# Seven quarter products in place of the full product in a projection, and where the conversions beside it run

## The chip, the cores and the metric

One core of a Trainium2 chip runs the whole program. Five engines work side by side on it: TensorE (PE, matrix products), VectorE (DVE, elementwise work and sums), ScalarE (ACT, activations and copies), GpSimd (POOL) and SyncE (SP, which only issues transfers here). Time is device time in microseconds (us) of one execution, the median of several.

## The reference

Two layers of attention over images of 512 channels and 32x32 = 1024 positions, for a batch of 8, all in 32-bit floating point:

```python
# layer 0: 8 heads
h = group_norm(xf, gn_w, gn_b)
q, k, v = split(einsum('oc,bct->bot', qkv_w, h) + qkv_b)   # per head
q, k, v = fake_quant(q), fake_quant(k), fake_quant(v)      # 8 bits, over the whole tensor
a = softmax(q * k * scale) @ v
x = xf + einsum('oc,bct->bot', proj_w, a) + proj_b         # the projection that is changed
# layer 1: 1 head of 512 channels
h = group_norm(x); q, k, v = h @ wq, h @ wk, h @ wv
x = x + (softmax(q k / sqrt(512)) v) wp + bp
```

## The kernel before, in words

A first stage (to about 570 us) computes q, k and v of layer 0 and their extremes. The rest is one long second stage. Its order is written out by hand: `attention()` is a generator that walks through layer 0's attention, image by image (8), pair of heads by pair (4), half of the positions by half (2) and 128 keys at a time (8); four such steps, called units, are one "advance". `others()` does for each image b the projection of layer 0 (`project`, line 1296), the group norm of layer 1 (`norm1`, line 1344) and layer 1's attention (`layer1`), and yields at chosen places; at each yield one advance of layer 0's attention is put between. So layer 0 of image b+2 runs beside layer 1 of image b. The instructions of TensorE, VectorE and ScalarE keep the order in which the program emits them. Nearly all of them are recorded under two helper lines: L209 is `mm`, every matmul, and L91 is the call through which every VectorE and ScalarE instruction goes; so groups are told apart by tile names.

In each unit TensorE makes scores (tile `st`, two PSUM banks), ScalarE takes their exponential (`pt`, 128x1024), one engine converts it to 16 bits (`two`), VectorE subtracts to get the low part (the other half of `two`, the group `two<-pt,two`), and TensorE multiplies both with v (`av`) and sums them (`sm`). For images after the first, the conversion is done on GpSimd for every fourth unit (line 1092) and on ScalarE for the rest. There are four `pt` buffers, so the exponential of unit u waits for the subtraction of unit u-4. An advance at u runs the products of units u to u+3 and the scores of units u+6 to u+9.

Work on VectorE that has time is put off by a small planner (`InOrder`, lines 89 to 157): `later` queues a chore under a name with a cost, a time when it is ready and one when it is due; `do` emits work that is wanted now, and first fills the gap before it with chores that fit; `settle` and `need` emit a chore at once because someone wants it. A chore is passed over if it would end more than 0.15 us after the gap:

```python
if begin + cost > limit + 0.15:
    continue
def elements(n):
    return 0.21 + n * 0.957e-3
```

`elements(512)` is 0.700 us, `elements(1024)` 1.190 us; a matmul of 256 columns counts 0.429 us. These figures only decide the order; the chip keeps its own time.

`project(b)` multiplies the 512x512 weights (tile `wp`) with image b's attention output (`ao`, four tiles of 128 channels x 2 halves x 512 positions). Per half it makes four outputs of 128 channels, each of four 128x128 by 128x512 products accumulated in one bank (`pj`); VectorE adds bank, bias and the input x into the tile `h` (`evict`), takes the statistics for layer 1's group norm (`stats`, a chore named "pj"), and SP stores the piece. Between the two halves lies one advance. For b = 0 the projection stands alone; for b = 1 to 7 it is put inside layer 1 of image b-1, in `o_run` (line 1540) after its fourth product, through `first` (line 1773): an advance ("the advance before"), half 0, an advance ("the middle one"), half 1, an advance in another order ("the late one": products of the first two units, then scores), then the norm. At b = 7 no attention is left, so the halves follow each other directly. In this place the banks `pj` are taken from the two buffers that the scores use (`score_bank`, line 315).

The norm averages over groups with a small matmul (`gps_b<-gmv_b,gavg`), which `more` (line 1781) emits right behind the fifth product of `o_run`, and a second one (`gps_b<-gd_b,gavg`) behind the sixth.

`seven` (line 1393) is the kernel's product by quarters in Winograd's form of Strassen's scheme: a product of 2x2 blocks with seven block products instead of eight, and sums of blocks before and after. Layer 1 uses it everywhere: tiles `g`, `v2ps`, `s` and `o` in the profile are its banks, two at a time, and each block product here is a number of 128x128 by 128x256 matmuls. `load_wp` (line 1266) fetches the projection's weights on ScalarE's queue, followed there by the image's x.

Of the kernel before, what the change touches and what calls it, by code (L numbers as in the profile page):

```python
# [18 lines left out]
P = 128  # L19
B, C, HH, WW = 8, 512, 32, 32  # L20
T = HH * WW
CC = C // P
# [36 lines left out]
def attn_pair_kernel(  # L59
# [166 lines left out]


    def norm_steps(
        src, dst, wcol, bank, nm, ccs=range(CC), fine=False, put=None, mv=None, apply=None
    ):  # L230

        n, c0 = len(ccs), ccs[0]
        put = put or (lambda hf, cost, work: work())
        if mv is None:
            st, mv = stat_tiles(n, nm)
            for i, cc in enumerate(ccs):
                for hf in range(NH):
                    dve.bn_stats(st[:, i, hf, :], src(cc, hf))  # L240
                aggregate(mv, st, i)
                if fine and i + 1 < n:
                    yield
        yield
        ps = bank(f"gps_{nm}")[:, 0:n]
        mm(ps, lhsT=gavg, rhs=mv[:, :, 0], start=True, stop=True)

        d = small.tile([P, n], F32, tag=f"gd{n}", name=f"gd_{nm}")
        mean = small.tile([P, n], F32, tag=f"gmean{n}", name=f"gmean_{nm}")

        def offsets():
            dve.tensor_sub(d, mv[:, :, 0], ps)
            dve.tensor_copy(mean, ps)
# [13 lines left out]
        if apply is not None:  # L267
            off = small.tile([P, n], F32, tag=f"goff{n}", name=f"goff_{nm}")
            dve.scalar_tensor_tensor(off, mean, -1.0, rstd, ALU.mult, ALU.mult)
            for i, cc in enumerate(ccs):  # L270
                apply(cc, rstd[:, i : i + 1], off[:, i : i + 1])
                yield
            return
        for hf in range(NH):
            for i, cc in enumerate(ccs):
                put(hf, 0.5, lambda i=i, cc=cc, hf=hf: dve.tensor_scalar(
                    dst(cc, hf), src(cc, hf), mean[:, i : i + 1], rstd[:, i : i + 1],
                    ALU.subtract, ALU.mult,
                ))
                if fine and i % 2 == 1:  # L280
                    yield
        if not fine:
            yield
# [23 lines left out]
    with ExitStack() as fast:  # L307
# [710 lines left out]
        def attention():  # L1018
# [44 lines left out]
            def split(u):  # L1063

                b, j, hf, s = units[u]
                pt, there = pts.pop(u)
                if not InOrder.planned:
                    for v in [v for v in put_off if v < u - 2]:
                        put_off.pop(v)()
                    deal(u)  # L1070
                else:
                    for v in list(put_off):
                        at_hand.add(v)
                        dve.later("sum", elements(1024), put_off.pop(v), pe.t, 9.0)
                if plain(b, s):
                    parts[u], ready[u] = pt, there
                    return
                two = partp.tile([P, 2, 2, 512], F16, tag="two", name=f"two_{b}_{j}_{hf}_{s}")
                parts[u] = two

                def rest():
                    dve.tensor_tensor(two[:, 1], pt, two[:, 0], ALU.subtract)
                    ready[u] = dve.t

                if u < BY_DMA and s in CAST_BY_DMA:
                    nc.gpsimd.dma_start(two[:, 0], pt)
                    put_off[u] = rest
                    return

                def cast(copy=act.copy):  # L1090
                    at_hand.add(u)
                    copy(two[:, 0], pt)  # L1092
# [64 lines left out]
            def finish(b, j, hf, u):  # L1157
# [106 lines left out]
                dma(xts[b][:, :, bass.ts(hf, 512)], x_v[b, :, :, bass.ts(hf, 512)])  # L1264

        def load_wp(b, dma):
            wps[b] = l2p.tile([P, CC, C], F32, tag="sums", name=f"wp0_{b}")
            dma(wps[b], w_sq[WP0])

        def load_first(u):  # L1270

# [21 lines left out]
            for t, src in zip(wm_tiles(b), wm_d):  # L1293
                act.dma_start(t, src)

        def project(b, bank=bank):

            settle("ao")  # L1300
            st, mvs[b] = stat_tiles(CC, f"b{b}")
            wp0 = wps.pop(b)
            for hf in range(NH):
                for oc in range(CC):
                    ps = bank(f"pj_{b}_{hf}_{oc}")
                    for cc in range(CC):
                        mm(
                            ps, lhsT=wp0[:, cc, bass.ts(oc, P)], rhs=ao[b, cc][:, hf, :],
                            start=(cc == 0), stop=(cc == CC - 1),
                        )  # L1310
# [33 lines left out]
        def norm1(b, bank=bank):  # L1344
# [14 lines left out]
                    put(hf, elements(512), work)  # L1359

            for n, _ in enumerate(norm_steps(
                at, at, V_GN1W, bank, f"b{b}", put=put, mv=mvs[b]
            )):
                if n == 2:
                    sums[b] = l2p.tile(
                        [P, 3, NH, CC // 2, 256], F32, tag="sums", name=f"sums2_{b}"
                    )
# [22 lines left out]
            dve.later("o", 0.25, spread, pe.t + 4.0, 5.0)  # L1390
            return rs

        def seven(nm, pairs, keep, whole, add, bank=bank):

            nonlocal turn
            turn ^= 1  # L1400
            x, y = (bank(f"{nm}_{i}").rearrange("p (t n) -> p t n", t=2) for i in range(2))

            def product(n, ps, start):
                left, right = pairs[n]
                k = left.shape[1]
                for t in range(2):
                    for i in range(k):
                        mm(
                            ps[:, t, :], lhsT=left[:, i, bass.ts(t, P)], rhs=right[:, i, :],
                            start=start and t == 0 and i == 0, stop=(i == k - 1),  # L1410
                            skip_group_check=True,
                        )
# [4 lines left out]
                (5, x, False, whole, None),  # L1417
            )
            for i, (n, ps, start, out, m) in enumerate(work):
                awaits(free[(i + turn) % 2])  # L1420
                product(n, ps, start)
                free[(i + turn) % 2] = out(ps) if m is None else out(m, ps)
                yield i + 1

        free = [0.0, 0.0]
        turn = 0

        def slots(gq):
# [235 lines left out]
        def layer1(b, steps):  # L1664
# [46 lines left out]
            for hf in range(NH):  # L1711
# [59 lines left out]
                if b + 1 < B and last:  # L1771

                    def first():
                        nonlocal ahead
                        yield -1
                        yield from project(b + 1, score_bank)
                        yield 2
                        ahead = norm1(b + 1, score_bank)
                        next(ahead)

                    def more():
                        next(ahead)
                        yield from ()

                    between = [first, more, more]
# [3 lines left out]
        def fold():  # L1789
# [36 lines left out]
            for i, (rows, lw, rw) in enumerate(((wa_rows, NQ1, NK1), (wm_rows, NV1, WP1))):  # L1826
# [74 lines left out]
        done = 0  # L1901
        dense = True
        late = False

        def advance():
            nonlocal done
# [407 lines left out]
```

## Time and profile before

| | |
|---|---|
| Median of 3 runs | 2557.06 us (2555.32 to 2558.21) |
| The profiled execution's own time | 2557.22 us |
| Its span, first to last instruction | 2555.4 us |
| Around the span | 1.8 us |
| TensorE busy | 2516.6 us (98%) |
| VectorE busy | 1895.6 us (74%) |
| ScalarE busy | 1348.2 us (53%) |
| GpSimd busy | 187.9 us (7%) |
| Mean granted TensorE clock | 0.999 |

Each row of the costliest groups reads: source line, engine, operation, output tile <- input tiles, shapes, count, then busy time and mean ns of one instruction, then how long the engine was idle just before these instructions and who ended that idle time. A 32-bit matmul stands in the trace as two instructions. Matmuls overlap, so busy time divided by the count is the spacing, and the mean of one is longer. The timeline merges neighbouring instructions of the same kind: start, duration, what, and in brackets the idle time before. The image b = 1 is taken as the sample: its projection starts at 930.9 us.

### The profile page before, as it was taken

How to read it: one execution, taken by the hardware profiler on the slowest of the kernel's cores; microseconds unless marked ns; L12 is line 12 of the kernel's file. 1: busy time of each engine (PE TensorE's matmuls, PEld its weight loads, DVE VectorE, ACT ScalarE, POOL GpSimd, SP SyncE). 2: the span in 40 equal slices, each digit the busy share in tenths (PEclk: the TensorE clock that was granted, in tenths of full speed). 3: DMA queues.
4: the chain of work that ended last, by engine and by line, in shares of the span. 5: the costliest groups of instructions: out<-in, count | busy, mean ns of one | idle time of the engine just before them, and what ended most of it. 6: DMA issues, size and time to landing. Idle time of an engine off the chain costs nothing.

```text
span 2555.4 us, 38727 instructions
## 1 busy us (share of the span) xinstructions
PE 2516.6 (98%) x15670; PEld 1746.1 (68%) x15670; DVE 1895.6 (74%) x2746; ACT 1348.2 (53%) x1687; POOL 187.9 (7%) x167
## 2 busy tenths in 40 slices
PE   8999999999999999999999999999999999999998
PEld 4788888873357756775777577657756775777687
DVE  7888776668887778777877787777778777775544
ACT  3332223219856655665667466656665675664122
POOL 0000000001100001000100100010101000100000
PEclk9999999999999999999999999999999999999999
DMA  4533333236622232223223222322232123212211
GB/s 167 178 142 124 132 124 121 110 130 164 164 88 63 79 113 87 59 70 127 92 59 104 84 87 74 109 96 63 80 109 91 55 72 124 87 51 84 87 38 39
DMA packets 160718, 250.70 MB, mean 98 GB/s; under 512 B 27153, under 2 KB 93713, under 8 KB 159121
## 3 DMA queue, kind: packets, MB, share of 16 engines
q1 hardware_dynamic: 125792, 182.81, 21.9%
q10 hardware_dynamic: 30560, 57.71, 6.6%
q0 software_dynamic: 4176, 7.60, 1.7%
q8 instruction: 125, 2.05, 0.3%
q14 instruction: 65, 0.52, 0.1%
HBM read 153.64 MB, written 86.28 MB: 94 GB/s over the span
## 4 chain that ended last, share of the span: by engine, by line
PE 85%; DVE 4%; issue 3%; ACT 2%; DMA 1%; POOL 0%; SPq 0%; ACTq 0%; DVEq 0%; POOLq 0%
PE s L209 15%; PE o L209 13%; PE qkps L209 12%; PE pj L209 8%; PE av L209 8%; PE v2ps L209 7%; PE g L209 6%; PE vps L209 6%; PE st L209 4%; PE sm L209 3%; ACT pt L91 1%; DVE two L91 1%; DVE h L91 1%; PE fold L209 0%; DVE acc L91 0%
## 5 line engine op out<-in xcount | busy, mean ns | idle before, releaser
L91 ACT ACTIVATE pt<-st,esc 128x1024 f32<-128x1024 f32 x467 | 497.1, 1115 | 332.7 <-PE st L209 316.8
L91 DVE TENSOR_TENSOR two<-pt,two 128x1024 f16<-128x1024 f32 x467 | 561.9, 1217 | 131.5 <-POOL two L1092 100.8
L91 ACT CAST two<-pt 128x1024 f16<-128x1024 f32 x346 | 350.8, 1056 | 6.9 <-ACT p L91 5.1
L1092 POOL CAST two<-pt 128x1024 f16<-128x1024 f32 x112 | 147.5, 1317 | 1406.8 <-PE sm L209 745.1
L209 PE MATMUL av<-two,v 128*32 128x512 f16 x3968 | 245.7, 381 | 2.5 <-DVE two L91 2.4
L209 PE MATMUL s<-g,h 128*128 128x256 f32 x1024 | 233.4, 380 | 0.0
L209 PE MATMUL pj<-ao,wp 128*128 128x512 f32 x512 | 224.0, 595 | 0.6 <-DVE h L91 0.6
L209 PEld LDWEIGHTS s<-g,h 128*128 128x128 f32 x1024 | 192.9, 190 | 31.0 <-issue 4.3
L91 ACT ACTIVATE u_ring<-qkps,qkbt 128x512 f32<-128x512 f32 x89 | 61.1, 687 | 243.6 <-PE qkps L209 228.9
L209 PEld LDWEIGHTS <-v 128*32 128x32 f16 x3968 | 92.0, 96 | 139.8 <-issue 66.7
L209 PEld LDWEIGHTS pj<-ao,wp 128*128 128x128 f32 x512 | 96.0, 190 | 122.5 <-issue 112.2
L209 PE MATMUL s<-g,sums 128*128 128x256 f32 x768 | 178.4, 381 | 0.2 <-DVE p L91 0.2
L209 PE MATMUL o<-p,v 128*128 128x256 f32 x768 | 175.2, 382 | 1.0 <-DVE p L91 1.0
L209 PE MATMUL st<-q,k 64*128 64x512 bf16 x1024 | 163.4, 382 | 12.2 <-ACT pt L91 7.8
L209 PEld LDWEIGHTS o<-p,v 128*128 128x128 f32 x768 | 144.3, 190 | 27.1 <-issue 5.7
L209 PEld LDWEIGHTS s<-g,sums 128*128 128x128 f32 x768 | 144.6, 190 | 24.3 <-issue 4.6
L209 PE MATMUL sm<-two,ones 128*32 128x512 f16 x1984 | 136.0, 379 | 0.0
L209 PEld LDWEIGHTS <-k 64*128 64x128 bf16 x1024 | 34.8, 94 | 144.1 <-issue 142.5
L209 PE MATMUL qkps<-half,w_high 128*128 128x512 f32 x480 | 132.5, 398 | 0.0
L209 PE MATMUL qkps<-half,w_mix 128*128 128x512 f32 x480 | 130.6, 394 | 1.0 <-DVE half L91 1.0
L209 PE MATMUL qkps<-half,w_low 128*128 128x512 f32 x480 | 130.5, 394 | 0.0
L209 PE MATMUL v2ps<-wm,h 128*128 128x256 f32 x512 | 119.9, 383 | 1.9 <-ACT g L91 1.3
(228 smaller groups left out, 3903.9 us busy)
## 6 DMA issues: line engine op xcount, KB each, us to landing
rs<-rs_d SPq DMA_DIRECT2D x76, 256.0 KB
x<-in_x_dram SPq DMA_DIRECT2D x32, 512.0 KB
q_d<-wa SPq DMA_DIRECT2D x32, 512.0 KB
k_d<-wa SPq DMA_DIRECT2D x32, 512.0 KB
v_d<-v_ring SPq DMA_DIRECT2D x32, 512.0 KB
raw<-q_d SPq DMA_DIRECT2D x32, 512.0 KB
raw<-k_d SPq DMA_DIRECT2D x32, 512.0 KB
x_d<-h SPq DMA_DIRECT2D x64, 256.0 KB
```

The costliest lines, as they stand in the source:

```text
L91: ins = self.latest = op(*args, **kw).ins
L209: ins = nc.tensor.matmul(ps, lhsT=lhsT, rhs=rhs, **kw).ins
L1092: copy(two[:, 0], pt)
```

## The change

For images 1 to 7 the projection is made by `seven` (`project_seven`); image 0 keeps the full product. While image 0 is projected, the four block sums of the weights are computed once (`combine_wp`) and all seven blocks are stored in device memory (`wp_d`). Later images load six blocks in one transfer into the buffer where the full weights stood (1.5 MB in place of 1 MB), and the seventh into a free part of layer 1's tile `v` (256 KB, on SP); that free part also takes two of the sums of the attention output. The other sums are formed in place in `ao`: one of them as a chore after the division of the second pair of heads (`first_sums`), the rest within each half. Each of the seven products is added by VectorE straight into the tile of x. The statistics are no longer settled at the end of the projection but after the late advance. The bias is taken out of the adding step: the norm's means are shifted by it (one small VectorE instruction more, ahead of the first averaging matmul) and it is added to layer 1's output bias. While the projection of images 1 to 6 runs, every fourth unit's conversion goes to ScalarE and not to GpSimd.

```diff
@@ norm_steps
+        if shift is not None:
+            dve.tensor_add(mv[:, :, 0], mv[:, :, 0], shift)
         ps = bank(f"gps_{nm}")[:, 0:n]
         mm(ps, lhsT=gavg, rhs=mv[:, :, 0], start=True, stop=True)
...
@@ split
-                elif s % 4 == 2:
+                elif s % 4 == 2 and not projecting:
                     cast(nc.gpsimd.tensor_copy)
...
@@ divide
                     dve.scalar_tensor_tensor(aot, aot, scl[:, 2:3], rs, ALU.mult, ALU.mult)
+                    if b and j == 1:
+                        first_sums(b)
...
@@ load_wp
-            wps[b] = l2p.tile([P, CC, C], F32, tag="sums", name=f"wp0_{b}")
-            dma(wps[b], w_sq[WP0])
+            wps[b] = w = l2p.tile([P, 6, CC // 2, C // 2], F32, tag="sums", name=f"wp0_{b}")
+            dma(w, wp_d[:, 0:6])
...
+        def first_sums(b):
+            for cc in range(CC // 2):
+                h = ao[b, cc]
+                dve.later("at", elements(512), lambda h=h: tt(
+                    h[:, :, 256:512], h[:, :, 256:512], h[:, :, 0:256], ALU.subtract
+                ), within=30.0)
+
+        def project_seven(b, room):
+            nonlocal projecting
+            projecting = True
+            settle("at")
             settle("ao")
...
+            nc.sync.dma_start(s4, wp_d[:, 6])
...
+            for k in range(2):
+                dve.do(elements(512), lambda k=k: second(k))
+
+            for hf in range(NH):
...
+                for step in seven(
+                    f"pj_{b}_{hf}",
+                    ((a11, h11), (a12, h21), (s2, th), (s3, h11), (s1, t1), (s4, h22), (a22, h21)),
+                    lambda n, ps: keeps[n](ps), into(q12, 0, 1, 1), lambda n, ps: adds[n](ps),
+                    score_bank, True,
+                ):
+                    if step in (1, 2):
+                        for k in range(2):
+                            h = (h11, h21)[step - 1][k]
+                            args = (h, th[k], h) if step == 1 else (h, h, th[k])
+                            dve.do(elements(256), lambda args=args: tt(*args, ALU.subtract))
+                    for oc in {6: (2, 3), 7: (0, 1)}.get(step, ()):
+                        dve.later("pj", 0.62 + 0.2 * hf, lambda oc=oc, stats=stats: stats(oc), within=4.0)
+                    chore()
+                if hf + 1 < NH:
+                    yield -1
...
@@ project (image 0)
-                        dve.scalar_tensor_tensor(
-                            xx, ps, vec[:, V_PB0 + oc : V_PB0 + oc + 1], xx, ALU.add, ALU.add
-                        )
+                        dve.tensor_tensor(xx, ps, xx, ALU.add)
...
@@ first, more
-                        yield from project(b + 1, score_bank)
+                        yield from project(b + 1, vt)
                         yield 2
+                        settle("pj")
                         ahead = norm1(b + 1, score_bank)
                         next(ahead)
...
                         next(ahead)
+                        projecting = False
...
@@ fold
                     dve.tensor_add(dst, tot, vec[:, V_BP : V_BP + CC])
+                    dve.tensor_add(dst, dst, vec[:, V_PB0 : V_PB0 + CC])
```

In `seven` the products come in the order 0, 1, 2, 3, 4, 6, 5 of the list, alternately into two banks x and y, beginning and ending with x. With the new argument `alone` its bank order starts afresh each time.

More of the change, by code (lines that the diff above doesn't have):

```diff
@@ L228, in norm_steps @@
     def norm_steps(
-        src, dst, wcol, bank, nm, ccs=range(CC), fine=False, put=None, mv=None, apply=None
+        src, dst, wcol, bank, nm, ccs=range(CC), fine=False, put=None, mv=None, apply=None,
+        shift=None,
     ):
@@ L252, in offsets @@
             dve.tensor_sub(d, mv[:, :, 0], ps)
-            dve.tensor_copy(mean, ps)
+            if shift is None:
+                dve.tensor_copy(mean, ps)
+            else:
+                dve.tensor_sub(mean, ps, shift)
             dve.tensor_mul(d, d, d)
@@ L1294, in load_wm, with combine_wp, keep @@
                 act.dma_start(t, src)
-        def project(b, bank=bank):
-            settle("ao")
+        wp_d = dram.tile([P, 7, CC // 2, C // 2], F32, tag="wp", name="wp_d")
+        def combine_wp():
+            wc = l2p.tile([P, 3, NT // 2, 256], F32, tag="vsum", name="wp_combined").rearrange(
+                "p a (s k) n -> p (a s) k n", k=2
+            )
+            a11, a12, a21, a22 = (
+                wps[0][:, k * CC // 2 : (k + 1) * CC // 2, m * 256 : (m + 1) * 256]
+                for m in range(2) for k in range(2)
+            )
+            s2, s3, s1, s4 = (wc[:, i] for i in range(4))
+            for args in (
+                (s1, a21, a22, ALU.add), (s2, s1, a11, ALU.subtract),
+                (s3, a11, a21, ALU.subtract), (s4, a12, s2, ALU.subtract),
+            ):
+                dve.later("wc", elements(512), lambda args=args: tt(*args), within=20.0)
+            def keep():
+                nc.sync.dma_start(wp_d[:, 3:7], wc[:, 0:4])
+            dve.later("wc", 0.0, keep, within=20.0)
+            nc.sync.dma_start(wp_d[:, 0], a11)
+            nc.sync.dma_start(wp_d[:, 1], a12)
+            nc.sync.dma_start(wp_d[:, 2], a22)
@@ new lines, in first_sums, with second, into, add @@
+        def first_sums(b):
[8 more added lines that the diff above has]
+            settle("at")
+            settle("ao")
+            st, mvs[b] = stat_tiles(CC, f"b{b}")
+            w = wps.pop(b)
+            a11, a12, a22, s2, s3, s1 = (w[:, i] for i in range(6))
+            t2 = room[:, 0 : NT // 2, 0:256].rearrange("p (k h) n -> p k h n", h=NH)
+            s4 = room[:, NT // 2 : NT // 2 + 2, 0:256]
+            nc.sync.dma_start(s4, wp_d[:, 6])
+            left, right = slice(0, 256), slice(256, 512)
+            def second(k):
+                tt(t2[:, k], ao[b, 2 + k][:, :, right], ao[b, k][:, :, right], ALU.subtract)
+            for k in range(2):
+                dve.do(elements(512), lambda k=k: second(k))
+            for hf in range(NH):
+                h11, t1, h21, h22 = (
+                    [ao[b, c + k][:, hf, n] for k in range(2)] for c in (0, 2) for n in (left, right)
+                )
+                th = [t2[:, k, hf] for k in range(2)]
+                q11, q12, q21, q22 = quarters(b, hf)
+                def into(q, row, col, full, hf=hf):
+                    def add(ps):
+                        there = dve.do(elements(512), lambda: tt(q, ps, q, ALU.add))
+                        if full is not None:
+                            nc.sync.dma_start(x1_d[b][row][hf][:, :, col * 256 : (col + 1) * 256], q)
+                        return there
+                    return add
+                def stats(oc, hf=hf):
+                    dve.bn_stats(st[:, oc, hf, :], xts[b][:, oc, bass.ts(hf, 512)])
+                    if hf == NH - 1:
+                        aggregate(mvs[b], st, oc)
+                keeps = [into(q, *at_, None) for q, at_ in ((q11, (0, 0)), (q21, (1, 0)), (q22, (1, 1)))]
+                adds = [into(q, *at_, 1) for q, at_ in ((q11, (0, 0)), (q21, (1, 0)), (q22, (1, 1)))]
+                for step in seven(
[3 more added lines that the diff above has]
+                    score_bank, True,
+                ):
+                    if step in (1, 2):
[8 more added lines that the diff above has]
+                    yield -1
+            for k in [k for k in ao if k[0] == b]:
+                del ao[k]
@@ L1301, in project @@
+        def project(b, room=None):
+            if b:
+                yield from project_seven(b, room)
+                return
+            settle("ao")
+            combine_wp()
             st, mvs[b] = stat_tiles(CC, f"b{b}")
@@ L1361, in norm1 @@
             for n, _ in enumerate(norm_steps(
-                at, at, V_GN1W, bank, f"b{b}", put=put, mv=mvs[b]
+                at, at, V_GN1W, bank, f"b{b}", put=put, mv=mvs[b], shift=vec[:, V_PB0 : V_PB0 + CC]
             )):
                 if n == 2:
+                    if b == 0:
+                        settle("wc")
                     sums[b] = l2p.tile(
@@ L1391, in inverse1, with seven @@
             return rs
-        def seven(nm, pairs, keep, whole, add, bank=bank):
+        def seven(nm, pairs, keep, whole, add, bank=bank, alone=False):
             nonlocal turn
-            turn ^= 1
+            turn ^= not alone
+            free, side = ([0.0, 0.0], 0) if alone else (busy, turn)
             x, y = (bank(f"{nm}_{i}").rearrange("p (t n) -> p t n", t=2) for i in range(2))
@@ L1408, in product @@
                         mm(
-                            ps[:, t, :], lhsT=left[:, i, bass.ts(t, P)], rhs=right[:, i, :],
+                            ps[:, t, :], lhsT=left[:, i, bass.ts(t, P)],
+                            rhs=right[i] if type(right) is list else right[:, i, :],
                             start=start and t == 0 and i == 0, stop=(i == k - 1),
@@ L1419, in seven @@
             for i, (n, ps, start, out, m) in enumerate(work):
-                awaits(free[(i + turn) % 2])
+                if not alone:
+                    side = turn
+                awaits(free[(i + side) % 2])
                 product(n, ps, start)
-                free[(i + turn) % 2] = out(ps) if m is None else out(m, ps)
+                free[(i + side) % 2] = out(ps) if m is None else out(m, ps)
                 yield i + 1
-        free = [0.0, 0.0]
+        busy = [0.0, 0.0]
         turn = 0
@@ L1781, in more @@
                     def more():
+                        nonlocal projecting
                         next(ahead)
+                        projecting = False
                         yield from ()
@@ L1903, in attn_pair_kernel @@
         late = False
+        projecting = False
         def advance():
```

## The prediction

> **What bounds the kernel now.** I read the engine totals and the chain that ended last first, then the groups of the projection, then the timeline around one projection (image 1).
>
> ```profile
> PE 2516.6 (98%) x15670; PEld 1746.1 (68%) x15670; DVE 1895.6 (74%) x2746; ACT 1348.2 (53%) x1687; POOL 187.9 (7%) x167
> ...
> L209 PE MATMUL pj<-ao,wp 128*128 128x512 f32 x512 | 224.0, 595 | 0.6 <-DVE h L91 0.6
> ```
>
> TensorE is busy 98% and the chain gives it 85%: less matmul time is less span, as long as TensorE is kept fed. The projections hold 224.0 us, 14.00 us for each of 16 halves. VectorE has 26% left on average, but the question is how much it has left there. So the timeline, TensorE first, image 1 (start, duration, what, idle before):
>
> ```profile
> 930.91 14.00 PE L209 MATMUL pj<-ao,wp 128*128 128x512 f32 x32
> 944.84 0.39 PE L209 MATMUL st<-q,k 64*128 64x512 bf16 x2
> 945.75 0.39 PE L209 MATMUL st<-q,k 64*128 64x512 bf16 x2 [0.52 <-DVE h L91]
> ...
> 947.49 0.60 PE L209 MATMUL st<-q,k 64*128 64x512 bf16 x4
> ...
> 963.36 1.05 PE L209 MATMUL av<-two,v 128*32 128x512 f16 x16
> ...
> 965.32 1.04 PE L209 MATMUL av<-two,v 128*32 128x512 f16 x16
> ...
> 967.27 3.72 PE L209 MATMUL o<-g,vsum 128*128 128x256 f32 x16
> 970.83 0.28 PE L209 MATMUL gps_b<-gmv_b,gavg 128*128 128x4 f32 x2
> 970.97 3.70 PE L209 MATMUL o<-g,v 128*128 128x256 f32 x16
> ```
>
> The only wait of note is 0.52 us at the middle advance: the scores take two buffers in turn, and the second is the last bank of half 0, still being added. At 970.83 the averaging matmul follows the product of `o` at once: its input was ready. VectorE in the same place:
>
> ```profile
> 960.71 1.22 DVE L91 TENSOR_TENSOR two<-pt,two 128x1024 f16<-128x1024 f32 x1
> 961.84 0.69 DVE L91 BATCH_NORM_STATS2 gst_b<-h 128x6 f32<-128x512 f32 x1
> 962.56 0.21 DVE L91 BATCH_NORM_AGGREGATE gmv_b<-gst_b 128x2 f32<-128x12 f32 x1
> 963.47 0.75 DVE L91 SCALAR_TENSOR_TENSOR h<-pj,vec,h 128x512 f32<-128x512 f32 x1 [0.70 <-PE pj L209]
> ...
> 967.03 1.23 DVE L91 TENSOR_TENSOR two<-pt,two 128x1024 f16<-128x1024 f32 x1 [1.83 <-POOL two L1092]
> 971.03 0.69 DVE L91 TENSOR_TENSOR kept_u<-o,kept_u 128x512 f32<-128x512 f32 x1 [2.78 <-PE o L209]
> 971.64 0.15 DVE L91 TENSOR_TENSOR gd_b<-gmv_b,gps_b 128x4 f32<-128x4 f32 x1
> ```
>
> Between two `h<-pj` lie 3.43 us, and VectorE fits one subtraction (`two`) and one set of statistics there, with idle time left. Three `two` run in each half (in half 1 at 954.81, 958.24 and 960.71).
>
> **Removed: matmul time.** A half is now 32 instructions of 512 columns, 14.00 us. It becomes 7 products x 4 matmuls x 2 = 56 of 256 columns. The nearest rows are blocks of the same form: the windows of tile `s` give 397.13 us for 1792, so 12.41 us per 56; those of `v2ps` 200.31 us for 896, so 12.52. By columns alone it would be 7/8 of 14.00, 12.25. I take `s`, the block with most instances: 1.59 us a half (1.48 to 1.75), times 14 halves = 22.3 us (20.7 to 24.5). Weight loads stay hidden: 0.190 us each beside a spacing of 0.222 us.
>
> Row against rule: the rows space matmuls by 0.437 us at 512 columns and 0.222 at 256, nearly the halving that the scheme needs. [...]
>
> **Added on VectorE, per image.** Fourteen additions from PSUM at 0.69 (the row at 971.03) for eight at 0.75: +3.7 us. Two sums of 512 before half 0 at 0.69: +1.4. Eight sums of 256, a form the trace lacks: 0.42 each by the line through 0.69 at 512 and 1.22 at 1024; the nearest rows of 256 are 0.35 (`vf<-raw`) and 0.51 (`x<-kept_u,ob,x`). So +3.4 (2.8 to 4.1). In all 8.5 us inside the stretch, and 1.4 (`first_sums`) some advances earlier. In the three windows 926.4 to 980.6 VectorE is busy 15.74, 12.26 and 10.21 of 54.1 us: 15.9 idle. The sum fits; its grain doesn't. An addition now comes every 4 x 0.429 = 1.717 us. The planner counts 0.700 for it, so the gap with its allowance is 1.017 + 0.15 = 1.167, and a `two` counts 1.190: it is passed over in every gap, by 0.02. Quantizations (0.7), statistics (0.62) and output steps (0.91) fit. So the `two` that now run within the halves are held back until `need` forces them, behind the last addition of the half. Inside a half TensorE should not wait: each bank is read within 0.9 us and wanted again after 1.72, and the quarter sums (two of 0.42 after the first and second addition) end before the product that reads them.
>
> **Added: waits of TensorE.**
>
> (a) *The first averaging matmul, 7 images.* The shift of the means is emitted behind the addition that follows the fifth product of `o`, and the matmul waits for it. Addition 0.20 after the product (970.83 to 971.03), next instruction 0.61 later (971.64), 0.15 for it, some 0.07 to TensorE: 1.03 us, 7.2 in all. It can't be much less; if VectorE is still behind, up to 2. Queued behind on TensorE: the sixth product.
>
> (b) *The late advance, 6 images.* Units 3 and 4 of those pending are wanted at 965.32. VectorE starts the last addition 0.11 after the products' end and the forced `two` 0.61 later; they follow at 1.17: the second ends at 0.72 + 1.17 + 1.22 = 3.11. TensorE wants it 1.96 + 0.49 (half of that group) = 2.45 after the end. With the signal 0.8 us, 4.8 in all; nothing if a gap takes the `two`, about 1.9 if exponentials, whose buffers these free, come late too.
>
> (c) *The middle advance, 6 images.* The first scores now take bank x, the last one written, not the second. Addition 0.11 + 0.69 and the signal: both scores come after 0.9, where now the second starts at 0.91: +0.3; the first exponential starts 0.9 later, and the scores at 947.49 wait for two of them: +0.2. I take 0.5, 3.0 in all (0.25 to 0.9).
>
> (d) *Image 7.* No advance lies between, so half 1 waits for x: 0.9 us.
>
> **Costed at nothing.** The conversions: 2 an image for 6 images, 1.07 us each on ScalarE, which is idle 23 us in this stretch; cover gone, 12.8 us. Weights: 0.5 MB more in front of x on ScalarE's queue; now 3.15 MB start at 907.95 and the windows show 364 GB/s to 919 and 32 after it, so 1.4 us more still leaves some 9 us. The seventh block on SP has 10 us until the seventh product. The stores are as many as before. `first_sums` lies in VectorE's 26%. Image 0: four sums (2.8 us) beside 27.05 busy of 33.1, and 1.75 MB stored; 0 to 1 us.
>
> A rule on GpSimd: at 928.45 a quantization took 1.49 us (median 0.748) while GpSimd converted; in the halves (947.12) it took 0.75. [...] If every one of the 12 conversions cost what the first row shows, VectorE would win 8.9 us, mostly ahead of no waiting matmul; by the second nothing. I take nothing.
>
> **Sum.** 22.3 - 7.2 - 4.8 - 3.0 - 0.9 = 6.4 us. The profiled execution took 2557.2 us (span 2555.4), 0.2 above the median: 2557.06 - 6.4 = 2550.7 us.
>
> **Rivals.**
>
> *The `two` find room* (planner times differ from my walk, say a cast is ready for the gap at a half's start). (b) goes and (c) falls to 0.25: 2550.7 - 4.8 - 1.5 = 2544.4 us. For it: 15.9 us idle. Against: 1.190 over 1.167.
>
> *VectorE's arrears run on; slower.* Behind the stretch lie the products of `g`, where the windows 980.6 to 1013 show VectorE busy 31.4 of 32.4 us, so it can't catch up. After the additions, 15.9 - 8.5 - 3.2 (shorter products) = 4.2 us are left in the stretch; each gap wastes some 0.3. If arrears beyond that force two `two` more per image onto TensorE's way (1.17 each), 14 us: 2565 us. It decides from 11.5 us, 1.9 an image.
>
> *Nothing waits*: 2557.06 - 22.3 = 2534.8 us. It needs (a) wrong, which the program's order speaks against.
>
> *The weights come late*: 9 us of lead speak against it; it would cost a wait ahead of half 0, some us for each image, and land at no change.
>
> **How the numbers follow.** My forecast 0.55; the `two` find room 0.20; arrears 0.16; nothing waits 0.03; weights or image 0 late 0.06. About 0.2% (5.1 us) is what a measurement can tell from no change: faster is under 2551.9, slower over 2562.2. The forecast's own range, with gain 20.7 to 24.5 and the waits' bounds, is 2546 to 2557 us; 0.33 of it lies faster and 0.22 within. So faster 0.33 + 0.20 + 0.03 = 0.56, same 0.22 + 0.06 = 0.28, slower 0.16. The range reaches to the first rival and part of the way to the second: 2543 to 2561 us.
>
> **What would show it.** Right: `pj` at 12.4 us a half in 784 instructions of 256 columns for seven images; `gps_b<-gmv_b` waiting about 1 us for the shift; no `two` inside a half but four behind half 1; `av` waiting for `two` 0.8 us in the late advance; the first `st` of the middle advance waiting 0.9 us. Wrong: `two` between the additions; products inside a half waiting for a quarter sum or for the weights; more idle time of TensorE at `g` or `v2ps`.

## The result, and the profile after

The changed kernel takes 2561.24 us (median of 20 runs, 2559.21 to 2562.59), the kernel before 2556.39 us beside it (20 runs, 2554.91 to 2559.03): a ratio of 1.0018, 95% interval 1.0011 to 1.0024. It is slower, by 4.9 us, where 6.4 us faster was forecast. The profiled execution took 2560.36 us (span 2558.6) against 2557.22 (span 2555.4), 3.1 us more; they lie 0.9 below and 0.8 above their medians, so what the traces account for is 3.1 of the 4.9 us.

First the page: TensorE's total, and the first of the projection's groups.

```profile
PE 2500.8 (98%) x16006; PEld 1809.7 (71%) x16006; DVE 1957.4 (77%) x2885; ACT 1362.7 (53%) x1699; POOL 172.1 (7%) x155
...
L209 PE MATMUL pj<-ao,wp 128*128 128x256 f32 (+1 forms) x624 | 155.2, 404 | 0.5 <-DVE h L91 0.5
```

TensorE has 15.8 us less to do and the kernel is no shorter: the gain was made and then spent on waiting. Where, the timeline of TensorE around the same projection tells (start, duration, what, idle before):

```profile
930.35 3.72 PE L209 MATMUL pj<-ao,wp 128*128 128x256 f32 x16
...
942.64 0.39 PE L209 MATMUL st<-q,k 64*128 64x512 bf16 x2
943.49 0.39 PE L209 MATMUL st<-q,k 64*128 64x512 bf16 x2 [0.46 <-DVE h L91]
...
945.83 0.39 PE L209 MATMUL st<-q,k 64*128 64x512 bf16 x2 [0.22 <-ACT pt L91]
...
962.96 0.40 PE L209 MATMUL av<-two,v 128*32 128x512 f16 x4 [0.34 <-DVE two L91]
...
969.15 0.36 PE L209 MATMUL gps_b<-gmv_b,gavg 128*128 128x4 f32 x2 [0.95 <-DVE gmv_b L91]
...
979.80 0.40 PE L209 MATMUL av<-two,v 128*32 128x512 f16 x4 [0.89 <-DVE two L91]
...
987.39 1.99 PE L209 MATMUL g<-h,wa 128*128 128x256 f32 x8 [0.41 <-DVE g L91]
```

A half lasts 942.64 - 930.35 = 12.29 us, where before it lasted 13.93. Then come six waits. The first stood there before, with 0.52 us. The next three lie where the prediction had priced one. The last two, at 979.80 and 987.39, lie behind the norm, where the prediction had nothing, and where the kernel before has no wait:

```profile
978.82 1.91 PE L209 MATMUL av<-two,v 128*32 128x512 f16 x32
...
987.38 1.99 PE L209 MATMUL g<-h,wa 128*128 128x256 f32 x8
```

VectorE in the changed kernel shows what is late:

```profile
960.56 4.62 DVE L91 TENSOR_TENSOR two<-pt,two 128x1024 f16<-128x1024 f32 x4
...
968.25 0.69 DVE L91 TENSOR_TENSOR kept_u<-o,kept_u 128x512 f32<-128x512 f32 x1 [0.63 <-PE o L209]
968.86 0.15 DVE L91 TENSOR_TENSOR gmv_b<-gmv_b,vec 128x4 f32<-128x4 f32 x1
...
978.53 3.48 DVE L91 TENSOR_TENSOR two<-pt,two 128x1024 f16<-128x1024 f32 x3
```

Four `two` behind half 1 and the shift (968.86) behind the addition, as forecast. But VectorE is idle for 0.63 us at 968.25 with nothing in hand, and ten microseconds later it runs three `two` in a row, for the first of which TensorE waits.

A measure that holds for all runs: each matmul outside `pj` stands in both kernels in the same order, so the shift of its start against the kernel before, taken at the borders of the stages, says in which stage time is won or lost. These are the means over images 1 to 6, in us per image, worked out from the traces of all the kernels told of below:

| stage | changed kernel | c1 | c2 | e1 | e2 | e3 | e5 | e6 | e7 | e8 |
|---|---|---|---|---|---|---|---|---|---|---|
| both halves | -3.29 | 0 | 0 | -3.29 | -3.29 | -3.29 | -3.29 | -3.29 | -3.29 | -3.29 |
| middle advance | 0.33 | 0 | 0 | 0.33 | 0.33 | -0.06 | 0.33 | -0.06 | 0.33 | -0.06 |
| late advance | 0.74 | 0 | 0 | 0.74 | 0.74 | 0 | 0.74 | 0 | 0.74 | 0 |
| first averaging matmul | 1.11 | 0 | 1.11 | 2.32 | 0 | 1.11 | 0.76 | 0 | 1.11 | 0 |
| rest of `o` | 0.08 | 0 | 0.07 | 1.48 | 0 | 0.08 | 0.07 | 0 | 0.08 | 0 |
| advance behind the norm | 1.07 | 1.39 | 0 | 0 | 1.27 | 2.86 | 0 | 0.55 | 1.07 | 0 |
| first `g` products | 0.46 | 0.46 | -0.22 | -0.22 | 0.46 | 0.55 | -0.16 | 3.85 | 0.46 | 2.01 |
| last matmul of the program | +1.4 | +11.1 | +6.1 | +6.9 | -6.9 | +6.9 | -11.2 | +4.0 | +0.8 | -11.6 |

In the changed kernel 3.79 us of waits stand against 3.29 us won, which loses 3.0 us in six images. Image 7, without an advance between its halves, wins 1.4 us (2.64 less 1.26 at the averaging matmul), and image 1 begins 0.6 us earlier; some 0.4 us is spread over the other stages, and the last matmul of the program comes 1.4 us later. The other 1.7 of the 3.1 us lie behind it: from its end to the end of the trace it is 7.24 us before and 8.98 after (see the last section).

### The profile page after: what moved, and what is told of

It reads as the page before. It is cut to its first block, busy times and chain, and to the rows that moved or that the text cites. A ratio compares the mean times of both kernels' runs of the same rounds, so it can differ in the third digit from the quotient of the medians.

```text
span 2558.6 us, 39591 instructions
## 1 busy us (share of the span) xinstructions
PE 2500.8 (98%) x16006; PEld 1809.7 (71%) x16006; DVE 1957.4 (77%) x2885; ACT 1362.7 (53%) x1699; POOL 172.1 (7%) x155
## 4 chain that ended last, share of the span: by engine, by line
PE 82%; DVE 7%; ACT 3%; DMA 2%; issue 2%; SPq 0%; POOL 0%; ACTq 0%; DVEq 0%
PE s L209 15%; PE o L209 12%; PE qkps L209 12%; PE v2ps L209 7%; PE av L209 7%; PE pj L209 7%; PE vps L209 6%; PE g L209 6%; PE st L209 4%; PE sm L209 3%; DVE two L91 3%; ACT pt L91 2%; DVE h L91 1%; PE fold L209 1%; DMA rs<-rs_d 1%
## 5 line engine op out<-in xcount | busy, mean ns | idle before, releaser
L91 ACT CAST two<-pt 128x1024 f16<-128x1024 f32 x358 | 362.0, 1054 | 9.7 <-issue 4.6
L1098 POOL CAST two<-pt 128x1024 f16<-128x1024 f32 x100 | 132.3, 1323 | 1208.9 <-PE sm L209 650.8
L209 PE MATMUL st<-q,k 64*128 64x512 bf16 x1024 | 165.5, 382 | 13.1 <-ACT pt L91 8.7
L209 PE MATMUL pj<-ao,wp 128*128 128x256 f32 (+1 forms) x624 | 155.2, 404 | 0.5 <-DVE h L91 0.5
L209 PEld LDWEIGHTS pj<-ao,wp 128*128 128x128 f32 x624 | 117.2, 190 | 35.4 <-issue 19.1
L209 PE MATMUL g<-h,wa 128*128 128x256 f32 x512 | 121.3, 385 | 2.5 <-DVE g L91 2.5
```

Of the source, the lines that this page charges most:

```text
L91: ins = self.latest = op(*args, **kw).ins
L209: ins = nc.tensor.matmul(ps, lhsT=lhsT, rhs=rhs, **kw).ins
```

## The experiments

Two theories were set against each other. **A**: VectorE has too much to do in the stretch, and whatever it is spared in one place comes back as a wait in another (the prediction's second rival). **B**: the conversion that moved to ScalarE stands there in a queue, so its subtraction `two` reaches VectorE's order too late for the place it had; VectorE's total work has little to do with it. Nine kernels were run beside the kernel before.

**c1: the kernel before, with the moved conversions alone.**

```diff
...
-                elif s % 4 == 2:
+                elif s % 4 == 2 and not projecting:
...
```

(`projecting` is set around the projection and the norm of images 1 to 6.)

> The kernel before with one part of the change alone: the full product stays, and in the projection's stretch every fourth unit (12 in all) is converted on ScalarE and not on GpSimd. Theory A: ScalarE idles 23 us there, so nothing is lost or won, within 2 us of before (ratio 0.9992 to 1.0008). Rival B: the fourth conversion in a row delays the fourth unit's two in the advance after the norm, 0.5 to 1.06 us an image: 3 to 6 us slower, 2559 to 2563 us.

2569.46 us (5 runs, 2568.37 to 2569.86) against 2556.38 (21 runs): 13.1 us slower, ratio 1.0051 (1.0037 to 1.0065), some 6 us above the range that B had expected. First GpSimd, ScalarE and VectorE in the kernel before, then the timelines of ScalarE, VectorE and TensorE in this run:

```profile
965.95 1.04 POOL L1092 CAST two<-pt 128x1024 f16<-128x1024 f32 x1 [17.18 <-ACT pt L91]
970.11 2.96 ACT L91 CAST two<-pt 128x1024 f16<-128x1024 f32 x3
975.85 1.21 DVE L91 TENSOR_TENSOR two<-pt,two 128x1024 f16<-128x1024 f32 x1
```

```profile
970.21 3.91 ACT L91 CAST two<-pt 128x1024 f16<-128x1024 f32 x4
971.12 0.69 DVE L91 TENSOR_TENSOR kept_u<-o,kept_u 128x512 f32<-128x512 f32 x1 [4.74 <-PE o L209]
...
976.03 1.22 DVE L91 TENSOR_TENSOR two<-pt,two 128x1024 f16<-128x1024 f32 x1
980.77 3.49 DVE L91 TENSOR_TENSOR two<-pt,two 128x1024 f16<-128x1024 f32 x3
...
982.04 0.40 PE L209 MATMUL av<-two,v 128*32 128x512 f16 x4 [1.44 <-DVE two L91]
```

An advance at u prepares four units (u+6 to u+9), and casts and `two` keep the order of the units, since the planner begins chores of one name in the order in which they were queued. In the kernel before, GpSimd converts the first of the four at 965.95, and VectorE runs its `two` at 967.03 (the prediction shows the line); the second unit's `two` comes at 975.85. Here the first unit's conversion heads a row of four casts that starts only at 970.21, behind four exponentials and two copies. VectorE is idle 4.74 us up to 971.12; the first unit's `two` then takes the second unit's place (976.03), and the second's goes behind the norm (980.77), where the products `av` wait 1.44 us for it. So the conversions alone cost 1.85 us an image at these two stages, 11.1 us up to the last matmul, and the two waits that the prediction lacked appear without any other part of the change. This is B, with a larger loss than it had expected. (The median is 2 us above what this trace shows, one execution among several.)

**e7: the changed kernel without the eight sums of 256 columns an image** (the products read unsummed quarters; 3.0 us less VectorE work an image by the changed kernel's rows, four pairs at 0.75).

```diff
...
-                    if step in (1, 2):
+                    if step in ():
...
```

> The changed kernel without the eight sums of 256 columns an image (the products read the unsummed quarters), so the output of images 1 to 7 is another; VectorE has some 3.4 us an image less to do within the halves, conversions stay on ScalarE. Theory A (arrears of VectorE set the waits behind the halves): the waits for `two` and `g` behind the norm and most of the late one go, 1.5 to 2.5 us an image, 2546 to 2552 us. Theory B (the subtraction waits for ScalarE's conversion, not for VectorE's time): those behind the norm stay at about 1.0 and 0.5 us an image, 2556 to 2561 us.

2561.53 us (11 runs, 2559.35 to 2562.80), ratio 1.0017 (1.0008 to 1.0026), the time of the changed kernel. TensorE's timeline:

```profile
962.58 0.40 PE L209 MATMUL av<-two,v 128*32 128x512 f16 x4 [0.34 <-DVE two L91]
...
979.42 0.40 PE L209 MATMUL av<-two,v 128*32 128x512 f16 x4 [0.89 <-DVE two L91]
```

The same waits to a hundredth of a microsecond, and the same column in the table. Taking work off VectorE inside the halves gives nothing back: A falls for that work.

**e1: the changed kernel with the conversions on GpSimd again.**

```diff
...
-                elif s % 4 == 2 and not projecting:
+                elif s % 4 == 2:
...
```

> The changed kernel with one part undone: in the projection's stretch every fourth unit is converted on GpSimd again, as before. Theory A (VectorE's arrears): what comes late behind the projection is VectorE, not the conversion, so the advance after the norm still waits about 1 us for two; time within 3 us of the changed kernel's 2561.2, ratio to before 1.001 to 1.003. Rival B (ScalarE's queue): four conversions in a row on ScalarE where there were three make the fourth unit's two later by one conversion, 1.06 us, which is just the wait seen (+1.06 us at the product of the fourth unit, 6 images): then 6 to 7 us come back, 2554 to 2555 us, and that wait is gone.

2565.87 us (5 runs, 2564.58 to 2569.85), ratio 1.0042 (1.0028 to 1.0055): 4.6 us slower than the change, above what either theory had expected. Taking back the part that c1 shows to cost 13 us makes it worse. VectorE and TensorE in its timeline:

```profile
960.48 5.46 DVE L91 TENSOR_TENSOR two<-pt,two 128x1024 f16<-128x1024 f32 x4
...
968.30 1.17 DVE L91 TENSOR_TENSOR two<-pt,two 128x1024 f16<-128x1024 f32 x1
969.39 0.68 DVE L91 TENSOR_TENSOR kept_u<-o,kept_u 128x512 f32<-128x512 f32 x1
...
970.29 0.36 PE L209 MATMUL gps_b<-gmv_b,gavg 128*128 128x4 f32 x2 [2.15 <-DVE gmv_b L91]
970.51 5.39 PE L209 MATMUL o<-g,v 128*128 128x256 f32 x16
```

And the row of its windows for the time just behind (busy time of each engine; TensorE's granted clock is the third number from the end):

```profile
971.70:975.10 3.40, 3.40 (x10) 2.65 (x9) 1.73 (x5) 0.00 (x0) 0.00 (x0) 0.50 0.24 72
```

Both waits behind the norm are gone (0 and -0.22 in the table). But now the first unit's `two` is ready early, and the planner puts it (968.30) in front of the addition and the shift; the averaging matmul waits 2.15 us instead of 0.95. Behind that wait the granted clock is 0.50 for 3.4 us, and the 16 instructions of `o` that took 3.70 us take 5.39. Five of the six images show such a window, at 1.7 us each some 8.5 us. The wait at the averaging matmul and this clock hide what the conversion costs.

**e2: the changed kernel with the shift of the means emitted right behind the statistics.**

```diff
...
-        if shift is not None:
+        if shift is not None and nm == "b0":
             dve.tensor_add(mv[:, :, 0], mv[:, :, 0], shift)
...
                         settle("pj")
+                        dve.tensor_add(
+                            mvs[b + 1][:, :, 0], mvs[b + 1][:, :, 0], vec[:, V_PB0 : V_PB0 + CC]
+                        )
...
```

> The changed kernel with the shift of the means emitted right behind the statistics, ahead of the addition that follows the fifth product of o (images 1 to 7). Theory (a): the averaging matmul no longer waits (1.11 us an image in the trace of the change, 1.18 at image 7): 7.8 us less, 2553.4 us, and the group gps_b<-gmv_b has no wait over 0.1 us. Rival: the time goes to the next wait, since VectorE is late anyway: the wait for two in the next advance grows by as much, and the time stays at 2558 to 2561 us.

2555.34 us (11 runs, 2552.15 to 2556.34), ratio 0.9995 (0.9986 to 1.0004): 5.9 us less than the change, from one instruction put elsewhere. The averaging matmul waits for nothing (0 in the table); the advance behind the norm takes 0.20 more. This is the price of term (a), less what comes back behind the norm (2 us short of the 7.8 that was expected).

**c2: the kernel before with one small VectorE instruction at that place** (the means copied onto themselves).

```diff
...
         yield
+        if nm in [f"b{i}" for i in range(1, B)]:
+            dve.tensor_copy(mv[:, :, 0], mv[:, :, 0])
         ps = bank(f"gps_{nm}")[:, 0:n]
...
```

> The kernel before with one small VectorE instruction (a copy of the 128x4 means onto themselves) ahead of the first averaging matmul of images 1 to 7, where the change has its shift. By term (a) of the prediction the matmul waits 1.03 us, 7.2 us in all: 2563.6 us. If the planner's subtraction comes in front, up to 2.2 us each: 2571. If something ahead hides it: 2556 to 2558.

2564.90 us (7 runs, 2563.43 to 2565.33) against 2557.09 (23 runs), ratio 1.0029 (1.0018 to 1.0041): 7.8 us for seven copies of some 0.15 us. TensorE's timeline:

```profile
971.18 0.36 PE L209 MATMUL gps_b<-gmv_b,gavg 128*128 128x4 f32 x2 [0.95 <-DVE gmv_b L91]
```

The same 0.95 as in the changed kernel. The cost is where the instruction stands in VectorE's order, not what it does.

**e3: the changed kernel with the planner's allowance at 0.30 while the projection runs**, so that `two` fits between two additions.

```diff
...
-                    if begin + cost > limit + 0.15:
+                    if begin + cost > limit + InOrder.allow:
...
             projecting = True
+            InOrder.allow = 0.3
...
```

> The changed kernel with the planner's allowance at 0.30 us in place of 0.15 while a projection of images 1 to 7 runs, so that a two (1.190) fits the gap between two additions (1.017 + allowance). Nothing else is changed. Theory A, in the strong form of the prediction (the grain of the gaps holds the two back, and that costs the late wait 0.72 us and the arrears 1.8 us an image): four two move into the halves, the late wait goes, and so does some of the arrears: 6 x 0.7 to 6 x 2.5, so 2546 to 2557 us. Rival A2 (VectorE has simply too much to do; what moves into the gaps pushes quantizations and output steps out, which then stand ahead of the same waits): the late wait goes (4.3 us), the waits behind the norm stay or grow, 2557 to 2561 us.

2559.91 us (11 runs, 2556.82 to 2566.01), ratio 1.0013 (1.0003 to 1.0022), not to be told from the change. The middle and the late wait are gone, as the first rival had it; the advance behind the norm then takes 2.86 us more in place of 1.07 (1.65 and 1.79 in the two images without a window of half clock, 2.85 to 4.02 in the four with one). The profiled execution (2566.01) has four windows of half clock and is the slowest of the 11, so the table shows more loss than the median does.

**e5: e1 and e2 together** (GpSimd's conversions and the early shift).

> The changed kernel with two edits: every fourth conversion on GpSimd again throughout, and the shift of the means emitted ahead of the chores, right after the statistics, so that the averaging matmul no longer waits behind a subtraction. Theory B (the conversion behind ScalarE's queue is what ate the gain; undone alone it only uncovered the wait at the averaging matmul): the waits for `two` and for `g` behind the norm go (some 1.6 us an image), the wait of the averaging matmul (1.1) goes too, no window of half clock is opened, and the time falls some 2.2 us an image below before plus the terms (b) to (d): 2541 to 2546 us. Theory A (VectorE's arrears, whoever converts): the time saved by the one returns as a wait at the next product, 2553 to 2560 us. If the clock windows come back with another wait over 2 us: above 2556.

2548.05 us (5 runs, 2546.98 to 2548.64) against 2557.09, ratio 0.9963 (0.9950 to 0.9977): 9.0 us faster than before and 13 us faster than the change; 2 us above the end of what B expected. TensorE and VectorE in its timeline:

```profile
969.55 0.17 DVE L91 TENSOR_TENSOR gmv_b<-gmv_b,vec 128x4 f32<-128x4 f32 x1
969.63 1.22 DVE L91 TENSOR_TENSOR two<-pt,two 128x1024 f16<-128x1024 f32 x1
969.86 0.36 PE L209 MATMUL gps_b<-gmv_b,gavg 128*128 128x4 f32 x2 [0.60 <-DVE gmv_b L91]
```

The `two` now stands behind the shift, both waits behind the norm are gone, and so is the half clock in the projections. Each edit alone left the other's wait, or made it larger: e1 gained -4.6, e2 5.9, both together 13.2 us. What stays is 0.60 us at the averaging matmul, since VectorE reaches the shift late: its four `two` behind half 1 take 5.46 us beside GpSimd's conversion, 4.62 without (e1's and the changed kernel's rows).

**e6: e5 with the allowance at 0.30.**

> As the run with both edits, and the planner's allowance at 0.30 instead of 0.15 while the projection runs, so that one subtraction `two` fits between two additions. Theory B: the middle and the late waits (0.4 and 0.7 us an image) go as well, 2536 to 2543 us. If the longer allowance pushes quantizations and output steps behind the norm as in the run with the allowance alone (+1.6 us an image there), it gives that back: 2545 to 2555 us.

2561.48 us (11 runs, 2557.80 to 2565.12), ratio 1.0016 (1.0007 to 1.0025): 13 us worse than e5, and over 6 us above both ranges expected. Middle, late and averaging waits are all gone. SyncE's queue (SPq, the issuing of transfers), VectorE and TensorE in its timeline:

```profile
968.39 0.33 SPq L980 DMA_DIRECT2D raw<-k_d  x1
968.81 1.19 SPq L1185 DMA_DIRECT2D apart<-rs  x2
973.32 0.17 DVE L92 TENSOR_TENSOR rcs<-apart 128x16 f32<-128x16 f32 x1 [3.90 <-DMA apart<-rs]
...
985.65 3.68 PE L210 MATMUL g<-sums,wa 128*128 128x256 f32 x8 [2.21 <-ACT vsum L92]
```

TensorE comes 2.0 us earlier to the end of `o` than in e5, but VectorE stands 3.90 us for the small transfer `apart<-rs`, with the second half of the norm behind it in its order. The norm is late, its sums are late, the product `g` waits 2.21 us, and the clock halves in five images.

**e8: e6 with those transfers issued from ScalarE's queue.**

```diff
...
-                    nc.sync.dma_start(
+                    (act if projecting else nc.sync).dma_start(
                         apart[:, w, :],
...
```

> The run with both edits and the larger allowance, but while the projection runs the two small transfers `apart<-rs` are issued from ScalarE's queue, right behind the copy that makes their source, and not from SP's, where an issue of 512 KB (`raw<-k_d`) that waits for a quantization stands in front of them. If VectorE's 3.90 us behind these transfers are what gave the larger allowance's gain back (the product `g` then waits 2.21 us for its sums, and a window of half clock follows): both go in six images, 2.2 x 6 = 13 us and some 8 us of half clock less, 2538 to 2544 us. If VectorE's work as such is what is late there: the wait at `g` stays over 1 us an image, 2550 to 2562 us.

2546.27 us (5 runs, 2544.86 to 2547.24) against 2556.96 (9 runs), ratio 0.9958 (0.9945 to 0.9972): the fastest of all, 10.7 us below the kernel before, but 2 us above the range expected. Its timeline:

```profile
970.86 0.17 DVE L92 TENSOR_TENSOR rcs<-apart 128x16 f32<-128x16 f32 x1 [2.86 <-DMA apart<-rs]
...
983.17 1.99 PE L210 MATMUL g<-sums,wa 128*128 128x256 f32 x8 [1.77 <-ACT vsum L92]
```

VectorE still stands 2.86 us for the transfer, and the wait at `g` fell only from 2.21 to 1.77 us. The expectation that it would go was wrong, and the time lies below the range of the other one, 2550 to 2562 us. About half of the 15 us against e6 is the clock: one window of half clock in the projections' images instead of five (some 7 us). The rest is the wait itself (with the clock's share, 2.01 us an image at the first `g` products in place of 3.85) and the advance (0 in place of 0.55).

## Why the prediction was wrong

**The failed step** is "Costed at nothing. The conversions: 2 an image for 6 images, 1.07 us each on ScalarE, which is idle 23 us in this stretch". Idle time in a stretch was taken for room at the moment when the conversion is wanted. Those 23 us are waits for the scores, nearly all of them ahead of the exponentials (11.91 us of them up to 964.77); then four exponentials, two copies and three casts already stood in a row. The conversion went in behind the copies, 4 us after GpSimd had made it (970.21 in c1, 965.95 before), and put the three casts and their `two` back by one place. It measured 1.07 + 0.46 = 1.53 us an image in the changed kernel, 9.2 us, and 11.1 us alone (c1, up to the last matmul). The stated cost "cover gone, 12.8 us" is near what was lost, but it priced TensorE waiting for every cast; what is lost is the place of `two` in VectorE's order.

**The terms that stood.** Gain: 1.59 us a half forecast, 3.29 / 2 = 1.645 measured, 23.0 us for 14 halves against 22.3. (a) the shift: 7.2 forecast; 1.11 for six images and 1.18 for image 7, 7.8 us, and 7.8 in c2, 5.9 back in e2. (b) the late advance: 4.8 forecast, 0.74 x 6 = 4.4. (c) the middle advance: 3.0 forecast, 0.33 x 6 = 2.0; of its detail the bank was wrong: the first scores did not wait, the second did (943.49), for 0.46 us where it had been 0.52, and the whole loss came with the wait for an exponential after it (945.83). (d) image 7: 0.9 forecast, 3.29 - 2.64 = 0.65. Together 23.0 - 7.8 - 4.4 - 2.0 - 0.65 = 8.1 us faster, close to the 6.4 of the sum. With the conversions' 9.2 and the 1.7 behind the last matmul, it is 2.8 us slower; the profiled execution was 3.1 slower. So the priced terms came out 1.7 us better than forecast in sum, and the conversions alone turn the sum round.

**GpSimd and VectorE together.** The prediction had one row that said a conversion on GpSimd slows VectorE and one that said it doesn't, and took nothing. e1 and the changed kernel give the price: four `two` 5.46 us beside a conversion and 4.62 without, 0.84 us, the same in all six images, and the conversion itself 1.90 us (1.04 where no `two` ran beside it, e6's timeline at 962.99). So moving the conversions does spare VectorE 0.84 us an image here, and loses 1.5.

**The rivals.** "The `two` find room" was no description of this order, but e3 made it come true and showed what the rival missed: the work that makes room goes behind the norm and is late there. "VectorE's arrears run on" came nearest in time (2565 us, on the slower side), and it named `two` on TensorE's way behind the stretch; but its mechanism, VectorE out of time, is refuted for the work in the halves by e7, where 3.0 us less changed nothing, and by c1, where VectorE has nothing added to it and idles 4.74 us ahead of the norm, and the `two` is late all the same. The weights caused no wait.

**What stays open.** Which of the two conversions an image costs the more was not tried apart; in c1 the stages from the first conversion up to the norm lose nothing (zeros in the table), which points to the second. In e8 VectorE waits 2.86 us for `apart<-rs` with the transfer already in ScalarE's queue; whether the norm's second half put in front of it would take the last 1.8 us was not tried.

## What to carry to other kernels

Idle time of an engine was no room for a moved step here (23 us idle, 1.53 us an image lost): look up what stands in that engine's queue when the step's input is ready, and which instruction behind it loses its place. An instruction of 0.15 us in front of a matmul cost what stood before it in its queue (here 1.1 us), so a late-emitted dependence is to be moved up before anything else is tuned. Two causes can cover each other: when undoing the suspected part makes the kernel slower (e1, by 4.6 us), look for the wait that took its place and undo both.

## What the hardware showed that was not expected

**The clock halved behind TensorE waits of about 2 us, and on a grid.** e1, e3, e6 and e8 have windows of 3.41 us at a granted clock of 0.50 in the projections' stretches, as in the row of e1 above, and c1 and e5 one at about 690 us. In e1 their starts lie 242.35, 242.35, 481.28 and 242.35 us apart, which are 71, 71, 141 and 71 times 3.4133 (481.28 / 141), the length of one window; those of e3 and e6 too lie whole multiples of it apart: in these traces they fall on a fixed grid. Counting TensorE's idle time (between the end of one matmul and the start of the next, from about 680 us on, all eleven traces) in each cell of that grid: the 16 cells with 1.88 us or more idle (1.88 to 2.81) were all followed by a cell at half clock; of the cells below, one of 1.71 us was, and those of 1.77, 1.73, 1.66 and less were not. So what decided it in these traces lay between 1.66 and 1.88 us of idle time, near half of a cell, and the same wait of 2.16 us in e1 went free in the one image of six where a border of the grid cut it into 0.43 and 1.73. Such a wait cost up to 1.7 us more than itself here (e1: 5.39 us in place of 3.70), by chance of its place.

**The end of the program is 1.7 us longer** in the changed kernel, where no work was changed: 7.24 us from the end of the last matmul to the end of the trace before, 7.25 in c1 and 7.30 in c2, but 8.98 after and 8.5 to 9.2 in all variants of the change. The last store is issued 1.54 us behind the last matmul in both; the difference lies between two of SyncE's closing semaphore instructions, which follow each other at 0.06 us before and at 1.76 us after. The trace doesn't name what fills that time: the last transfer counted by the semaphore named there had landed 9.8 us before the end of the last matmul. It wasn't tried; it is a third of the 4.9 us by which the change is slower.
